# A selective-scan kernel: turning y between tiles, early weights and fillers in the head, last sums ahead of the last epilogue step, and one more step in the preparation of delta

## Chip, cores and metric

The kernel runs on one core of one Trainium2 chip. The metric is the device time of one execution in microseconds (us), as the median of several executions. In the profile, PE is TensorE, PEld its weight loads, DVE VectorE, ACT ScalarE, POOL GpSimd and SP SyncE; SPq is the queue of DMAs that SP issues.

## The reference, cut to what matters

The input is x [4, 64, 64, 96] in f32: four images, here called batches. A first block projects x to 2 x 192 channels with sign weights (`W_in`), puts one half through a 3x3 convolution of signs and a SiLU, and runs a selective scan over the 4096 pixels in four directions (by rows, by columns, and both reversed):

```
delta = softplus(delta + delta_bias)
dA = exp(dt[..., None] * A[None])
h  = dA * h + (dt * ut)[..., None] * Bt[:, :, None, :]
y  = einsum('bkdn,bkn->bkd', h, Ct)
return y + D[None, :, :, None] * u
...
inv_y = flip(out_y[:, 2:4], axis=-1)
y = out_y[:, 0] + inv_y[:, 0] + wh_y + invwh_y
y = (y - mu) / sqrt(var + 1e-05) * ln_w + ln_b
y = y * silu(z)
return bilinear(y, W_out, s_out, b_out)
```

h has 16 states for each of 192 channels. B, C and the input of delta are sign projections of the convolved image (`Wl`, then `Wd` for delta). Two column directions give y in transposed order (`wh_y`, `invwh_y`), so their sum has to be turned before it is added to that of the rows. Behind the block come an attention without softmax (its k and v are summed over all pixels of a batch before any output can be made) and a feed-forward layer whose operands are rounded to 8-bit floats.

## The kernel before, in words

**Work of a batch.** A batch is a *prologue*, 384 scan *pieces* and an *epilogue*.

- `prologue` (L539) takes group means, projects x (L647, L648), and convolves the signs in 16 parts of 512 pixels. A part is 15 matmuls L745 and one L786 that adds the input (`cz`); DVE and ACT finish it as u, stored to DRAM by rows (`ud`) and by columns (`utd`). Then the *rows stage* transposes the signs of u (`xa`, `xb`, L874), projects them with `wR` (`acc`, L940), and stores B and C (`bcd`, L952) and the signs for delta (`sgd`, L953). These are loaded again as `g` (L965) and turned (`gp`, L975) into `gT`.
- A piece is a tile [128 x 1024]: 32 channels by 4 of the 16 states, over 1024 pixels. The directions come in the order KORD = (1, 3, 0, 2), 96 pieces each: columns forwards and backwards, then rows. A batch is 384 pieces, the kernel 1536.
- The epilogue has `sums` (L1152) with eight tiles of 512 pixels (norm, gate, output projection, share of the attention's sums), `middle` (L1297), which makes a small matrix of the sums, and `last` (L1311), again eight tiles, which makes the output.

**The loop over pieces.** `Scans.run` (L1722) is an order written out by hand; step i issues:

1. `loads(i)`: B, C (`bc`, L1520) and delta (`dl`, L1531) by DMAs of 512 KB on SP; at every fourth piece the further summands of y (`load_sums`, L1611).
2. `carry(i-1)` (L1597), which keeps the last column of a scan, and `decay(i+1)` (L1554), exp of delta times A into PSUM, both on ACT. There are two decay buffers.
3. At every eighth step `evacuate(i-5)` (L1642): ACT copies finished y out of PSUM.
4. `reduce(i-4)` (L1628, L1633): PE sums products over the states into a bank of y; banks `y0` and `y1` alternate, one for every eight pieces.
5. `inject(i+3)`: POOL multiplies delta*u by B into a buffer `w`. `late_product`: POOL's product with C for an earlier piece, if it was left to POOL.
6. `scan(i)`: DVE's scan, and either DVE's product with C or none. Which engine takes the product is decided by `Tally` (helper L443), a running sum of estimated costs of each engine; it is kept from the start of the program.
7. DMA stores that are due, a step of `prepare`, and one step of the generator `back`.

`prepare` (L1450) makes a part of delta in steps, one per piece, starting at every eighth: matmuls L1489 into the bank of y that is not being summed, then Abs and Relu (L1494, L1495), Exp and Ln (L1497, L1498), a matmul L1502 that adds, DVE's product with u, ACT's copy L1508 out of the bank, and stores. The first reduce of the next eight pieces needs the bank free.

`back` (L491) runs all other work behind the pieces, one step at each: prologues of batches 1 to 3, epilogues of batches 0 to 2, and the *turns*. `turn(c, b)` (L994) loads the summed column directions of batch b in 16 tiles (`yt`), copies each in turned order on ACT (`yh`, L1015) and stores them in two DMAs (L1022). In `back` the turn of batch b+1 stands after all `sums` tiles of batch b, if its columns are nearly done by then, or else after the whole epilogue of b. The rows' directions of a batch need its turned y: when `run` comes to them (KORD 2) and it isn't turned, it runs `back` until it is, and issues no piece meanwhile.

**Head and tail.** For batch 0 the prologue runs alone, interleaved with `weights` (L163), a generator that loads, signs and transposes the weights; each of its transposes is a PE matmul into a y bank and a copy. `Scans.start` (L1668) then makes the first delta and its spread copies (`dl_s`, L1711). The last batch's epilogue runs alone too (`alone`), on two further lanes (`ln0`, `ln1`) and later a fourth (`l4`).

Of the kernel before, what the change touches and what calls it, by code (L numbers as in the profile page):

```python
# [25 lines left out]
CH = 1024  # L26
# [27 lines left out]
def hybrid_kernel(ctx: ExitStack, tc: tile.TileContext, a: dict, out: bass.AP):  # L54
# [108 lines left out]
    def weights():  # L163
# [39 lines left out]

        wi = temp("wi", [128, 3, DM], F32)
# [19 lines left out]
        wl = [temp(f"wl{o}", [128, DN], F32) for o in range(2)]  # L224
        for o in range(2):
            nc.gpsimd.memset(wl[o], 0.0)
            for kk in range(2):
                k, r0 = o + 2 * kk, 64 * kk
                nc.sync.dma_start(wl[o][r0 : r0 + 32, :], a["wl_bc"][32 * k : 32 * k + 32, :])
                nc.sync.dma_start(wl[o][r0 + 32 : r0 + 32 + NR, :], a["wl_dt"][k])  # L230
        wd = [temp(f"wd{x}", [128, NK, NR], F32) for x in range(2)]
        nc.sync.dma_start(wd[0], a["wd"][0:128])
        for r0 in (0, 64):
            nc.sync.dma_start(wd[1][r0 : r0 + 64], a["wd"][128:DN])
        wo = temp("wo", [DM, DN], F32)
        nc.sync.dma_start(wo, a["w_out"])
        small = {}
# [22 lines left out]
        nc.vector.tensor_tensor(sbx, pvx[:, :, B_X], pvx[:, :, MOVE0], ALU.add)  # L260
        wim = negmean("wim", wi, DM)
        wis = temp("wis", [128, 3, DM], BF16)
        for t in range(3):
            nc.scalar.activation(wis[:, t, :], wi[:, t, :], AF.Sign, bias=wim[:, t : t + 1])
        ps = transposed(winT, [wis[:, t, :] for t in range(3)])
        for x in range(2):
            nc.vector.tensor_copy(winB[:, 64 * x : 64 * x + 64], ps[0:DM, 128:DN], saturate=False)
        yield
        for i, cut in enumerate(cuts):
            nc.scalar.activation(cwA.rearrange("p t d -> p (t d)")[:, cut], cfa[i], AF.Sign, saturate=False)  # L270
            nc.scalar.activation(cwB[:, lines[i]], cfb[i], AF.Sign, saturate=False)
        yield

        part = temp("part", [96, 2, 2])
        for i in range(2):
            for h in range(2):
                nc.vector.tensor_reduce(part[:, h, i : i + 1], cwn[h][i], AX.X, ALU.add, apply_absolute_value=True)
            yield
        nc.vector.tensor_tensor(csc, part[:, :, 0], part[:, :, 1], ALU.add)
        nc.vector.tensor_scalar(csc, csc, 1.0 / (9 * DN), None, ALU.mult)  # L280

        nc.vector.tensor_tensor(cbias, pv[:, :, CONV_B], pv[:, :, RP0], ALU.add)
        nc.vector.tensor_tensor(acs, pv[:, :, PRELU], csc, ALU.mult)
        nc.vector.tensor_tensor(acb, pv[:, :, PRELU], cbias, ALU.mult)
        nc.vector.tensor_tensor(acb, acb, pv[:, :, B_X], ALU.add)
        nc.vector.tensor_tensor(acb, acb, pv[:, :, RP1], ALU.add)
        nc.vector.tensor_scalar(oma, pv[:, :, PRELU], -1.0, 1.0, ALU.mult, ALU.add)
        for h in range(2):
            nc.gpsimd.tensor_scalar(omad[:, h], i96, oma[:, h : h + 1], None, ALU.mult)
        yield  # L290

# [3 lines left out]
        kinds = (((0, 1), (2, None), (None, 0), (1, 2)), ((1, 0), (None, 2), (0, None), (2, 1)))  # L295
        for o in range(2):
# [5 lines left out]
            for kk in range(2):  # L302
                rows = slice(64 * kk, 64 * kk + 64)
                for x, pair in enumerate(kinds[kk]):
                    for half, j in enumerate(pair):
                        if j is not None:
                            to, src = we[rows, x, 64 * half : 64 * half + 64], sw[rows, 64 * j : 64 * j + 64]
                            if o:
                                to = we[rows, x, half::2]
                            else:  # L310
                                to, src = to.rearrange("p (e i) -> p i e", e=2), src.rearrange("p (i e) -> p i e", e=2)
                            nc.gpsimd.tensor_copy(to, src)
            yield
            yield
            transposed(wR[:, o].rearrange("p x m -> p (x m)"), [we[:, x, :] for x in range(4)])
            yield


        wdt = []
        for x, t in enumerate(wd):  # L320
            wdm = negmean(f"wdm{x}", t, NR)
            wds = temp(f"wds{x}", [128, NK, NR], BF16)
            for k in range(NK):
                nc.scalar.activation(wds[:, k, :], t[:, k, :], AF.Sign, bias=wdm[:, k : k + 1])
            wdt.append(temp(f"wdt{x}", [NR, NK * 32]))
            yield
            transposed(wdt[x].bitcast(F8), [wds[:, k, :] for k in range(NK)])
            yield
# [4 lines left out]
        for r0 in (0, 64):  # L333
            for s in range(8):
                at = r0 + NR * s
                nc.sync.dma_start(wdy.bitcast(F32)[at : at + NR, :, s, r0 // 4 : r0 // 4 + 16], two[:, :, 0:16])
        yield
        nc.vector.tensor_tensor(dbias, pvd[:, :, NK : 2 * NK], pvd[:, :, 2 * NK :], ALU.add)
# [3 lines left out]

# [3 lines left out]
        transposed(woutT.rearrange("p h m -> p (h m)"), [wos[:, 96 * h : 96 * h + 96] for h in range(2)])  # L346
        yield
        nc.vector.tensor_scalar(mean[:, 0], i96, -1.0 / DN, None, ALU.add)
        nc.vector.memset(mean[:, 1], -1.0 / DN)

        ones, diag = temp("ones", [96, 128]), temp("diag", [96, 4, 96])
        nc.vector.memset(ones, 1.0)
        for i in range(2):
            for h in range(2):
                col = pv[:, h, (LN_W, LN_B)[i] : (LN_W, LN_B)[i] + 1]
                nc.gpsimd.tensor_scalar(diag[:, 2 * i + h], i96, col, None, ALU.mult)
        yield
        ps = p.ps.tile([128, 512], F32, name="tpw", tag="y1")
        nc.tensor.matmul(ps[:, 0:384], ones, diag.rearrange("p i m -> p (i m)"), start=True, stop=True)
        for h in range(2):  # L360
# [8 lines left out]
        nc.vector.tensor_copy(  # L369
            back4.rearrange("p (x d) -> p x d", x=4), ident.rearrange("p (x d) -> p x d", x=4)[:, ::-1, :]  # L370
        )
# [11 lines left out]
        nc.vector.memset(on192, 1.0 / DN)  # L383
        nc.vector.memset(on96, 1.0 / DM)
        nc.vector.tensor_scalar(mean96, i96, -1.0 / DM, None, ALU.add)
        yield
        for name, dst in (("w1", w1q), ("w2", w2q), ("b1", b1q), ("b2", b2q)):
            q = dst if dst.dtype == F8 else temp(name + "q", list(dst.shape), F8)
            nc.vector.tensor_copy(q, small[name], saturate=False)
            if q is not dst:  # L390
                nc.vector.tensor_copy(dst, q)
        yield
        for k in range(NK):
            o, r0 = k % 2, 64 * (k // 2)
            nc.sync.dma_start(sbR[r0 : r0 + 32, o, 0:1], a["sl_bc"][0:32, k : k + 1])
            nc.sync.dma_start(sbR[r0 : r0 + 32, o, 1:2], a["bl_bc"][:, 32 * k : 32 * k + 32].rearrange("o p -> p o"))
            nc.sync.dma_start(sbR[r0 + 32 : r0 + 32 + NR, o, :], a["sl_dt"][k])
        yield
        al, al2 = temp("al", [128, 2, NK * NS]), temp("al2", [128, 2, 4, NK * NQ])
        nc.sync.dma_start(al, a["al"].rearrange("p h k s -> p h (k s)"))  # L400
        yield
        nc.scalar.activation(al, al, AF.Exp)
        nc.vector.tensor_scalar(al2, al.rearrange("p h (s j) -> p h j s", j=4), -1.0, None, ALU.mult)
        for g in range(NG):
            nc.sync.dma_start(anm[:, g, :], al2[32 * (g % 4) : 32 * (g % 4) + 32, g // 4])

    c = SimpleNamespace(**locals())
    c.ready, c.turned, c.later = set(), set(), Later(nc)
# [18 lines left out]
def load_x(c, b, xts):  # L427
    src = c.a["x"][b].rearrange("(i p) e -> p i e", p=128)
    for q, t in enumerate(xts):
        c.nc.sync.dma_start(t, src[:, 8 * q : 8 * q + 8, :])  # L430

# [40 lines left out]
def run(c):  # L472
# [6 lines left out]
    for _ in range(6):  # L479
# [11 lines left out]
    def back():  # L491
# [3 lines left out]
        for b in range(NB):  # L495
# [9 lines left out]
            if b + 1 < NB:  # L505
                if scans.done(b + 1, 2, 20):
# [21 lines left out]
    more.append(e.fourth_lane())  # L528

# [9 lines left out]
def prologue(c, b, xts=None):  # L539
# [11 lines left out]
    with tc.tile_pool(name=f"xg_{b}", bufs=1) as xgp:  # L551
# [3 lines left out]
        with tc.tile_pool(name=f"cv_{b}", bufs=1) as cvp:  # L555
# [23 lines left out]

            csum = bank("csum", 0)[0:1, 0 : 4 * DM]  # L580
# [153 lines left out]
            def alone_parts():  # L734

                mid = end = None
                for n, part in enumerate(parts + [None, None]):
# [4 lines left out]
                    for s in range(4):  # L742
# [17 lines left out]
                        elif s == 2:  # L760
                            if ahead:
                                next(ahead.pop(0), None)
                            if mid:
# [17 lines left out]
                    if part:  # L781
# [6 lines left out]
                        )  # L788
                        mid = (h, q, pz, v, r, nm)
# [65 lines left out]
        with tc.tile_pool(name=f"rw_{b}", bufs=1) as rw:  # L855
            xrs = rw.tile([128, 96, 64], BF16, name=f"xr_{b}", tag="xr")

            g2 = rw.tile([128, 2, 384], F8, name=f"g_{b}", tag="g")
            gw = g2.bitcast(F32)
# [6 lines left out]
            for o in (1, 0):  # L866
# [29 lines left out]

                for gh in range(2):
# [49 lines left out]
                    for kk in range(2):  # L947
                        k, r0 = o + 2 * kk, 64 * kk
                        for x, t in enumerate(tbcs):
                            n = L // 2 // len(tbcs)  # L950
                            at = L // 2 * gh + n * x
                            nc.sync.dma_start(c.bcd[b][k][:, at : at + n], t[r0 : r0 + 32, :])  # L952
# [3 lines left out]
                        )  # L956
                    if fast and gh == 0:
                        c.first_u()
                    yield
                c.later.flush()  # L960
                if o:
                    nc.gpsimd.memset(gw[:, :, 0:16], 0.0)
                    nc.gpsimd.memset(gw[:, :, 64:96], 0.0)
                for x, k in enumerate((o, o + 2)):
                    nc.sync.dma_start(gw[:, x, 16:64], c.sgd[b][k].rearrange("(p f) -> p f", p=128))  # L965
                    if fast and x:
# [873 lines left out]
```

## Time and profile before

| What | Value |
|---|---|
| Times of three runs, median | 5361.95 us (5360.22 to 5364.72) |
| The profiled execution | 5356.94 us |
| Its span, first to last instruction | 5355.2 us |
| Mean granted TensorE clock | 0.737 |
| First convolution matmul | 30.8 us |
| First scan | 180.2 us |
| POOL product, DVE scan, DVE product | 2.35, 2.34, 1.23 us |
| ACT decay | 1.12 us |
| ACT copy of the turn, L1015 | 1.07 us |

A line of the timeline gives start, duration, engine, source line, operation, output <- inputs, shapes and count (alike instructions next to each other are put together), and in brackets how long the engine had been idle before it and what ended that. A line of waits gives total, number and longest. The page's slices give the busy share in tenths of 40 equal pieces of the span, 134 us each. The granted clock is the share of full speed at which TensorE was allowed to run. Much of DVE's and POOL's work has the helper's line L443, so it is told apart by its tiles.

### The profile page before, as it was taken

Reading aid. Unit: us, or ns where it says so; the run is one execution under the profiler, and the core shown is the slowest. Engines: PE = TensorE matmul, PEld = TensorE weight load, DVE = VectorE, ACT = ScalarE, POOL = GpSimd, SP = SyncE. Lnnn points to the kernel's source line nnn. Section 1 sums busy time; section 2 is a strip of 40 time slices with the busy share of each in tenths; the row PEclk is TensorE's granted clock in tenths of the full one; section 3 lists DMA queues with packets and bytes.
Section 4 is the critical chain, followed back from the end, with each engine's and each line's share of the span. In section 5 each row is a group of like instructions: output and inputs, shape, how many; then the busy total and the mean of one; then the engine's idle time right before and its main releaser. Section 6 shows DMA issues by size and latency. Waiting matters only on the chain. (4 is left out here: it accounts for less than half of the span.)

```text
span 5355.2 us, 61897 instructions
## 1 busy us (share of the span) xinstructions
PE 3387.5 (63%) x20029; PEld 1351.6 (25%) x20029; DVE 5004.4 (93%) x3168; ACT 3606.7 (67%) x5644; POOL 4951.9 (92%) x2254
## 2 busy tenths in 40 slices
PE   7457665567645666566676556775666676664577
PEld 3212222122222222222222222222222222221223
DVE  4699999999999999999999999997999999999995
ACT  6577767687766666677777766666776666776554
POOL 4699999999999999999999999998999999999990
PEclk8667776678866877677777768776777776676788
DMA  5666666867766666766666666666666566667652
GB/s 107 189 194 197 212 189 203 260 203 211 222 195 182 205 218 203 230 208 204 216 204 193 193 207 224 195 198 222 201 204 211 189 209 202 200 190 233 217 177 65
DMA packets 605594, 1068.83 MB, mean 200 GB/s; under 512 B 219771, under 2 KB 336916, under 8 KB 603540
## 3 DMA queue, kind: packets, MB, share of 16 engines
q1 hardware_dynamic: 602884, 1063.93, 63.7%
q8 instruction: 157, 2.57, 0.2%
q14 instruction: 169, 1.38, 0.1%
q0 software_dynamic: 1536, 0.79, 0.1%
q10 hardware_dynamic: 848, 0.15, 0.0%
HBM read 829.69 MB, written 228.30 MB: 198 GB/s over the span
## 5 line engine op out<-in xcount | busy, mean ns | idle before, releaser
L443 POOL TENSOR_TENSOR w<-dl,bc 128x1024 f32<-128x1024 f32 x1524 | 3549.5, 2355 | 60.3 <-PE yp L1628 43.7
L1554 ACT ACTIVATE dA<-dl,anm 128x1024 f32<-128x1024 f32 x1524 | 1701.3, 1116 | 511.9 <-DVE w L443 319.0
L443 DVE TENSOR_TENSOR_SCAN dA<-dA,cy,w 128x1024 f32<-128x1024 f32 x726 | 1700.7, 2343 | 61.3 <-ACT dA L1554 50.1
L443 POOL TENSOR_TENSOR w<-h,bc 128x1024 f32<-128x1024 f32 x570 | 1341.4, 2353 | 100.5 <-DVE h L443 95.5
L1628 PE MATMUL yp<-w,sum 128*32 128x256 f32 x12288 | 1230.4, 500 | 157.4 <-ACT pd L1508 109.4
L443 DVE TENSOR_TENSOR w<-dA,bc 128x1024 f32<-128x1024 f32 x966 | 1183.3, 1225 | 63.8 <-DMA bc<-bcd 1.9
L443 DVE TENSOR_TENSOR_SCAN h<-dA,cy,w 128x1024 f32<-128x1024 f32 x426 | 996.8, 2340 | 3.4 <-ACT dA L1554 3.1
L1597 ACT COPY cy<-dA 128x1 f32<-128x1 f32 x723 | 114.2, 158 | 829.1 <-DVE w L443 828.1
L1628 PEld LDWEIGHTS yp<-w,sum 128*32 128x32 f32 x12288 | 320.0, 127 | 1218.4 <-issue 741.0
L443 DVE TENSOR_TENSOR_SCAN dA<-dA,w 128x1024 f32<-128x1024 f32 x240 | 547.7, 2282 | 50.8 <-ACT dA L1554 48.2
L443 DVE TENSOR_TENSOR_SCAN h<-dA,w 128x1024 f32<-128x1024 f32 x144 | 328.1, 2279 | 9.0 <-POOL w L443 8.6
L1489 PE MATMUL dps<-gT,wdz 128*128 128x64 fp8e5 x1008 | 115.5, 314 | 323.8 <-ACT ys L1642 313.8
L1502 PE MATMUL dps<-sp,ident 128*128 128x512 f32 x378 | 266.4, 793 | 73.1 <-ACT dps L1498 72.7
L1633 PE MATMUL yp<-ya,back 128*128 128x256 f32 x576 | 225.6, 511 | 0.0
L1489 PEld LDWEIGHTS <-wdz 128*128 128x128 fp8e5 x1008 | 94.5, 152 | 402.2 <-issue 401.3
L806 PE MATMUL cv<-tp,cwA 128*96 128x512 fp8e5 x432 | 160.2, 492 | 43.1 <-ACT r L838 41.8
L1597 ACT COPY cy<-h 128x1 f32<-128x1 f32 x429 | 79.9, 186 | 158.9 <-DVE h L443 158.6
L1489 PE MATMUL dps<-gT,wdy 128*128 128x64 fp8e5 x504 | 57.0, 312 | 183.1 <-ACT ys L1642 182.8
L1280 PE MATMUL kv<-wkv,tt 97*128 97x192 f32 x240 | 76.8, 491 | 136.9 <-DVE tt L443 136.9
L1494 ACT ACTIVATE pd<-dps,dbias,pvd 128x512 f32<-128x512 f32 x189 | 144.0, 762 | 20.9 <-PE dps L1489 20.6
L1143 PE MATMUL yc<-eys,mean 96*96 96x512 f32 x240 | 133.5, 708 | 35.6 <-DVE vks L443 21.4
L1633 PEld LDWEIGHTS yp<-ya,back 128*128 128x128 f32 x576 | 118.9, 238 | 119.3 <-issue 88.6
(380 smaller groups left out, 4559.2 us busy)
## 6 DMA issues: line engine op xcount, KB each, us to landing
dl<-dld SPq DMA_DIRECT2D x762, 512.0 KB
bc<-bcd SPq DMA_DIRECT2D x512, 512.0 KB
dld<-pd SPq DMA_DIRECT2D x126, 512.0 KB
yd<-ys SPq DMA_DIRECT2D x764, 64.0 KB
dld<-pd SPq DMA_DIRECT2D x126, 256.0 KB
ya<-yd SPq DMA_DIRECT2D x192, 128.0 KB
pu<-ud SPq DMA_DIRECT2D x32, 512.0 KB
pu<-utd SPq DMA_DIRECT2D x31, 512.0 KB
```

What stands on the lines that cost most here:

```text
L443: return getattr(self.eng, name)(out, *args, **kw)
L806: nc.tensor.matmul(ps, w[:, 96 * h : 96 * h + 96], tp[:, 8 * q + dy : 8 * q + dy + 8, dx : dx + IW], start=(w is taps[0][1]), stop=(w is t ...
L1143: self.c.nc.tensor.matmul(ps, w, x, start=(i == 0), stop=(i == len(pairs) - 1))
L1280: nc.tensor.matmul(pk[i // 2][:, i % 2], tt[:, 128 * i : 128 * i + 128], c.wkv, start=True, stop=True)
L1489: nc.tensor.matmul(pv[:, s], wd[:, k, s], gT[:, :, c0 : c0 + 16], start=(s == 0), stop=(s == 7))
L1494: nc.scalar.activation(d[:, 0], ps, AF.Abs, scale=sc, bias=bi)
L1502: nc.tensor.matmul(ps, c.ident, t, start=False, stop=True, skip_group_check=True)
L1554: c.nc.scalar.activation(t, self.dlt[i // NQ][0], AF.Exp, scale=c.anm[:, g, NQ * KORD[e] + q : NQ * KORD[e] + q + 1])
L1597: self.c.nc.scalar.copy(self.carries[g, q], h[:, CH - 1 : CH])
L1628: c.nc.tensor.matmul(y[32 * x : 32 * x + 32, g % 2, :], c.sum4, prod[:, 256 * x : 256 * x + 256], start=(q == 0), stop=(q == NQ - 1 and no ...
L1633: c.nc.tensor.matmul(y[:, g % 2, :], w, src, start=False, stop=(n == len(more) - 1))
```

## The change

1. **Turn between tiles.** A new method `between` is called by the main lane of `sums` and by `last` ahead of each tile. If the columns of the next batch are done, it turns them there.
2. **Head, weights.** The loads of `wl` and `wd` come first and on ACT's queue; their signs and transposes (`wR`, `wdt`) come before the first projections. `al` is loaded early; the loads of `sbR` and `anm` move up. The transposes of `woutT` and the matmuls `tpw` and `tpd` are deferred until all projections of the prologue are issued (`c.projected`). The 16 loads into `wdy` go to POOL's queue.
3. **Head, rows stage.** Stores of `sgd` go ahead of those of `bcd`. The first u and the first eight `bc` loads go to POOL's queue, right after the first half of the rows. Two memsets move up. The two tallies are set to zero when the pieces begin.
4. **Fillers.** `keep_busy` issues matmuls whose result nobody reads: 24 behind the last part of the convolution, 20 before the `gp` columns, 4, 2 and 2 in `middle` of the last batch and 4 and 3 in the first tile of `last`; 8 more ahead of the first group mean.
5. **End.** At the last piece `back` is not stepped, so the four last reduces and the last evacuation come ahead of the next epilogue step. By the instruction order, the main lane's tile 2 of the last batch is then made in the form for a lone epilogue, with two matmuls for the mean in place of eight.
6. **prepare.** One more `yield` between the matmuls L1489 and their use.

Cut to its core:

```diff
@@ weights
+                nc.scalar.dma_start(wl[o][r0 : r0 + 32, :], a["wl_bc"][32 * k : 32 * k + 32, :])
...
+        nc.scalar.dma_start(wd[0], a["wd"][0:128])
...
+        for x, t in enumerate(wds):
+            transposed(wdt[x].bitcast(F8), [t[:, k, :] for k in range(NK)])
...
+            if i == 0:
+                for o in range(2):
+                    transposed(wR[:, o].rearrange("p x m -> p (x m)"), [wes[o][:, x, :] for x in range(4)])
+                yield
...
+        while not c.projected:
+            yield
+        transposed(woutT.rearrange("p h m -> p (h m)"), [wos[:, 96 * h : 96 * h + 96] for h in range(2)])
@@
+def keep_busy(c, ps, n):
+    for _ in range(n):
+        c.nc.tensor.matmul(ps, c.identb, c.wR[:, 0].rearrange("p x m -> p (x m)"), start=True, stop=True)
@@ run
-    for _ in range(6):
+    for n in range(6):
+        if n == 4:
+            next(made)
         next(first)
@@ back
-                if scans.done(b + 1, 2, 20):
+                if b + 1 not in c.turned and scans.done(b + 1, 2, 20):
@@ prologue, rows stage
-                            nc.sync.dma_start(c.bcd[b][k][:, at : at + n], t[r0 : r0 + 32, :])
+                            rest.append((c.bcd[b][k][:, at : at + n], t[r0 : r0 + 32, :]))
...
+                    if not (fast and gh):
+                        for pair in rest:
+                            nc.sync.dma_start(*pair)
+                        rest.clear()
                     if fast and gh == 0:
                         c.first_u()
+                        c.loads_ahead()
...
+                if fast:
+                    keep_busy(c, c.p.ps.tile([128, 512], F32, name="warm_rw", tag="y1"), 20)
...
-                    if fast and x:
-                        c.loads_ahead()
@@ Epilogue
+            if ln is self.lane:
+                yield from self.between()
...
+    def between(self):
+        b = self.b + 1
+        if not self.alone and b < NB and b not in self.c.turned and self.scans.done(b, 2):
+            yield from turn(self.c, b)
@@ Scans.prepare
         yield
+        yield
@@ Scans.first_loads
-        for w, to in enumerate((self.bt, self.ct)):
-            for q in range(NQ):
-                self.load_bc(w, to, 0, 0, 0, q)
+        for w, q in ((0, 0), (1, 0), (0, 1), (0, 2), (0, 3), (1, 1), (1, 2), (1, 3)):
+            self.load_bc(w, (self.bt, self.ct)[w], 0, 0, 0, q, self.c.nc.gpsimd)
@@ Scans.run
+        c.vec.us = c.gps.us = 0.0
...
-            next(back, None)
+            if i < n - 1:
+                next(back, None)
```

## Prediction

> **What bounds the kernel now.** I read the busy shares first, then the slices, then the waits, and last the timeline of every stretch in which VectorE (DVE) stood still.
>
> ```profile
> PE 3387.5 (63%) x20029; PEld 1351.6 (25%) x20029; DVE 5004.4 (93%) x3168; ACT 3606.7 (67%) x5644; POOL 4951.9 (92%) x2254
> DVE  4699999999999999999999999997999999999995
> POOL 4699999999999999999999999998999999999990
> ```
>
> DVE and GpSimd (POOL) are both full from the third slice to the last but one: 1536 pieces at about 3.27 us each, with POOL products of 2.35 us, DVE scans of 2.3 and DVE products of 1.23. An edit shortens the kernel only if it takes DVE and POOL idle time away, or shortens the head (before the pieces) or the tail (after them). There are three such places: slices 1 and 2, the 7 in the middle, and the last slice.
>
> The middle one, from the timeline around 3670 us:
>
> ```profile
> 3670.24 7.72 ACT L1015 COPY yh<-yt 96x512 f32<-96x512 f32 x8 [8.83 <-DMA yt<-yd]
> 3679.14 2.30 DVE L443 TENSOR_TENSOR_SCAN dA<-dA,w 128x1024 f32<-128x1024 f32 x1 [23.96 <-ACT dA L1554]
> 3681.08 2.36 POOL L443 TENSOR_TENSOR w<-dl,bc 128x1024 f32<-128x1024 f32 x1 [20.05 <-PE yp L1628]
> ```
>
> The turn's copies stand in ScalarE's (ACT) queue ahead of the next decay, waiting for loads. DVE stops for 24.0 us, POOL for 20.1. It is the only turn of the four that does so.
>
> The head, from the timelines of TensorE (PE), SyncE's queue (SP), ACT and DVE:
>
> ```profile
> 86.54 1.46 PE L745 MATMUL cv<-tp,cwB 128*96 128x512 fp8e5 x6
> 97.43 0.59 PE L786 MATMUL cz<-xsT,winT 96*96 96x512 fp8e5 x1 [9.44 <-DVE u L443]
> ...
> 157.65 1.03 PE L975 MATMUL gp<-ident,g 128*128 128x128 fp8e5 x8 [11.30 <-DMA g<-sgd]
> ...
> 156.86 5.67 SPq L1520 DMA_DIRECT2D bc<-bcd x8
> ...
> 175.98 2.15 ACT L1554 ACTIVATE dA<-dl_s,anm 128x1024 f32<-128x1024 f32 x2 [7.24 <-DMA dl_s<-w_s]
> ...
> 191.50 2.29 DVE L443 TENSOR_TENSOR_SCAN h<-dA,w 128x1024 f32<-128x1024 f32 x1 [6.28 <-POOL w L443]
> ```
>
> The convolution has 16 parts, each with one L786 matmul, and these start at 36.58, 41.31, 49.20, 58.42, 62.33, 70.91, 79.93, 83.84, 97.43, 103.94, 107.86, 111.86, 117.20, 120.68, 124.51 and 127.98. Undisturbed parts come 3.9 us apart, which 15 intervals would make 58.7; they take 91.4. The excess of 32.7 is weight preparation run between the parts.
>
> The tail, from PE's timeline and a table by stretches (busy us of PE, PEld, DVE, ACT, POOL with counts; clock; DMA):
>
> ```profile
> 5236.83 6.85 PE L1143 MATMUL yc<-eys,mean 96*96 96x512 f32 x8 [2.86 <-DVE vks L443]
> 5243.61 1.93 PE L1628 MATMUL yp<-w,sum 128*32 128x256 f32 x32
> ```
>
> ```profile
> 5285.00:5312.00 27.00, 23.59 (x33) 6.56 (x34) 9.04 (x18) 10.33 (x17) 0.00 (x0) 0.56 0.27 79
> 5312.00:5332.00 20.00, 17.07 (x83) 9.25 (x82) 12.96 (x26) 15.00 (x26) 0.00 (x0) 1.00 0.11 30
> ```
>
> The last sums of y wait behind 6.8 us of an epilogue tile, and the first round of the last layer runs at half clock.
>
> **The turn.** In the instruction order the third turn moves from pieces 1055–1057, where 14 of its copies form one burst, to 975–994, a copy per piece, and the fourth from 1406–1425 to 1358–1377. What 16 spread copies cost can be read from the turns that are spread already: in the 20 pieces of the first turn DVE's idle gaps over 0.05 us sum to 1.8 us, in those before and after to 2.5 and 0.9; in the fourth to 0, against 1.6 before it. So the copies of 1.07 us hide under ACT's idle third, and the 16 loads and 2 stores on SP come some 60 pieces before y is needed. Without that cover they cost at most 16 x 1.07 = 17 us again. The stall goes: the 10 pieces around it took 54.9 us instead of 33, so **−22** (20 to 24). Next due is only the following decay.
>
> **The head up to the convolution's end.** The transposes of wR and wdt go ahead of the first projection, and the work behind `al` (the 9.44 above: DVE waits for an ACT copy of it, which waits for its load) starts earlier. The intervals that end at 41.31, 49.20, 58.42, 97.43, 103.94 and 117.20 lose their excess: 0.8 + 4.0 + 5.3 + 9.7 + 2.6 + 1.4 = 23.8. Those ending at 70.91 and 79.93 hold the transposes of woutT, tpw and tpd (4.7 + 5.1), which the change only defers to when all projections are done, near part 11; I keep their cost. So −24 (−30 if they fit there, −12 if half of it returns). Against it, the early work stands before the first projection (24.01 us): eleven weight loads issued by ACT with waits, 2.6 us of signs, two copies of 0.68 and two of 0.42: +5 (+3 to +9).
>
> **From rows to the first pieces.** The sgd stores went out at 152.03 and 154.24 behind bcd stores; in front of them they leave some 3.5 us earlier. But the 8 bc loads (512 KB each) now start ahead of the g loads, on POOL's queue, and share the engines with these: I take −2 (−4 to +3). In return bc is out of the way when dl_s loads: those took 8.2 us to the first decay at a DMA share of 1.0 (158 to 180 us); at 5 us less crowding −4 (0 to −6). The Trainium skill, "DMA: Bandwidth & Descriptors", section "Issuing engine by pattern", speaks against this queue: a simple load belongs on Sync, GpSimd being slower, some 0.4 us to the first byte by the page's figures. The trace has 5.67 us for 8 issues on SP, 0.71 each, and 0.49 each for POOL's three xg issues. By the page +0.4 once, by the row nothing, since POOL is idle then; I take the row. The tallies set to zero give the first pieces' products to DVE: the waits of 6.28 and 2.32 us on POOL before scans 2 and 3 shrink by about −3.5. Fillers: 24 wide matmuls after the last part at 0.3 us (the bf16 pair of 512 columns took 0.59) are 7 us under PE's idle 7.4 before xa; 20 are 6 to 11 us (0.55 each at the slow clock) under the 11.3 shown: nothing, at worst +5.
>
> Head: −24 + 5 − 2 − 4 − 3.5 = **−28** (−10 to −40).
>
> **The tail.** With the reduces ahead of the epilogue step they start at 5236.8 instead of 5243.6: −6.8. The main lane's tile 2 of the last batch then takes the short mean, with up to 3.9 us of yc, sy and var less before the means of lanes 0 and 1: −10.7 in all; its eight additional DVE operations (0.64, 0.43, 0.74, 0.69, twice each) are 5.0 us, of which 3.5 on the path. Clock: fv takes 2.02 us at 5289 and 1.10 at 5321. Twelve such pairs lie in the slow stretch, 11 us; half is then covered by DVE and ACT, so −5.5. Here a rule disagrees with the row. The Trainium skill, "TensorE: Matmul & The Clock Gate", section "Part 1: The HAM clock gate", lets the clock drop after an idle window of about 3.4 us and return after a busy one of that length. In the row PE idles 0.8 us at a time at most, is 87% busy, and stays at 0.56 for 27 us. By the rule no gap asks for fillers: gain 0, cost 15 x 0.3 less PE's 2.9 us of gaps, +2. By the row density decides, and fillers buy 5.5. I take the row, less the cost. Tail: −10.7 + 3.5 − 5.5 + 2 = −10.7, taken as **−10** (−2 to −17).
>
> **The steady pieces.** Four more products on DVE: 4 x 1.23 = +5. Pieces whose decay must wait out a scan (about 65 gaps of 1.25 us) are 62 in the new order: −4. The additional step in prepare moves the copy L1508 one step (3.3 us) later, in ACT's queue, and the reduces behind it on PE:
>
> ```profile
> PE yp L1628 <- ACT pd L1508: 109.4, 29, 7.0
> ```
>
> Where that bank's reduce began less than 3.3 us after the copy it slips, 1.8 us on average. A late reduce hurts only if POOL then waits for its w buffer; carrying each slip against the slack to the inject nine pieces later, 13 of about 190 pay, 12 us in all; with one buffer more, none. I take +3 (0 to +12). ACT's wait of 20.6 us for PE before L1494 goes, but ACT is not the bound: 0. Together **+4**.
>
> **Sum.** −22 − 28 − 10 + 4 = −56. The profiled execution took 5356.94 us (span 5355.2): 5301. The median, 5361.95, stands 5.0 above it: **5306**.
>
> **Rivals.**
> 1. *The head gives little.* For it: the page of slices has DMA at 0.5 to 0.7 here, and new ACT issues precede everything. If early loads cost +9, half the excess returns (−12), and g is late by 3, the head is −12+9+3−4−3.5 = −7.5: 5326.
> 2. *Slower: the late copy empties the ring of w buffers.* If the slack is one step shorter than I count, the same sum gives 67 late injects and 88 us: 5306 − 3 + 88 = 5391. It decides from 0.3 us per prepare (59 / 189). Against it: POOL's waits for yp are 43.7 us now, 20 of them in the one stall.
> 3. *The fillers don't do what they say*: the clock stays at half, or they stand before needed matmuls: tail −4, rows +3: 5315.
> 4. *The turn's copies only move the stall*: −5 instead of −22: 5323.
>
> **How the numbers follow.** Forecast 0.60 (5288 to 5318), rival 1 0.15, rival 2 0.05, rival 3 0.10, rival 4 0.04, a head and tail at their best ends (5280) 0.06. Range 5280 to 5330. About 0.2% (11 us) is what the measurement tells from no change. Faster 0.94; the same 0.03, where several rivals meet; slower 0.03, rival 2 less the part of it that stays under the others' gain.
>
> **What would show it.** Right: no DVE gap over 10 us after 205; first scan near 155 to 160; L786 intervals of 3.9 except two; last reduces right after the last product; clock near 1.0 through the first round. Wrong: POOL waiting over 60 us for yp, or the intervals still above 5.

## The result, and the profile after

The changed kernel takes 5290.6 us (median; 5288.3 to 5294.7) against 5361.1 us before, a ratio of 0.9868 (95% interval 0.9851 to 0.9885), so 70 us less. 5306 was forecast, with 5280 to 5330 as the range. The profiled execution took 5288.32 us, its span 5286.5, which is 68.6 us less than before.

From the page after, busy shares and slices of 132 us:

```profile
PE 3427.5 (65%) x20089; PEld 1358.7 (26%) x20092; DVE 5011.1 (95%) x3178; ACT 3606.5 (68%) x5644; POOL 4956.0 (94%) x2277
...
DVE  5799999999999999999999999999999999999996
...
POOL 5799999999999999999999999999999999999991
```

The 7 in the middle of DVE's row is a 9, and the second slice went from 6 to 7; busy times grew by 7 and 4 us. What was taken away is idle time.

I lay the starts of equal scans side by side and get this account (a minus is earlier than before):

| Stretch | Before | After | Change | Forecast |
|---|---|---|---|---|
| Start to the convolution's first L786 (after: L804) matmul | 36.58 | 42.26 | +5.7 | +5 |
| From there to the last of the 16 | 91.4 | 67.0 | −24.4 | −24 |
| From there to the first scan | 52.2 | 52.2 | 0.0 | −6 |
| First scan to scan 5 | 21.6 | 17.9 | −3.7 | −3.5 |
| Scans 1050 to 1100, with the turn | 186.3 | 161.5 | −24.8 | −22 |
| All other pieces | | | −8.1 | +4 |
| Last product to the end | 118.5 | 105.2 | −13.3 | −10 |

The head after, from the timelines of PE and DVE:

```profile
109.26 0.38 PE L804 MATMUL cz<-xsT,winT 96*96 96x512 fp8e5 x1
109.48 5.34 PE L440 MATMUL warm_cv<-wR,identb 128*128 128x512 bf16 x23
...
136.71 0.62 PE L1008 MATMUL gp<-ident,g 128*128 128x128 fp8e5 x8 [2.11 <-DMA g<-sgd]
141.41 0.61 PE L1008 MATMUL gp<-ident,g 128*128 128x128 fp8e5 x4 [4.07 <-DMA g<-sgd]
...
161.47 2.30 DVE L453 TENSOR_TENSOR_SCAN dA<-dA,w 128x1024 f32<-128x1024 f32 x1
```

The fillers lie where PE waited. But there are now two waits for g, where there was one of 11.3 us before. The queue of SP shows that nothing stood between the two loads before, and four bcd stores after:

```profile
155.79 1.03 SPq L965 DMA_DIRECT2D g<-sgd  x2
```

```profile
130.86 0.35 SPq L1000 DMA_DIRECT2D g<-sgd  x1
131.30 1.97 SPq L1020 DMA_DIRECT2D bcd<-tbc  x4
133.37 0.46 SPq L1000 DMA_DIRECT2D g<-sgd  x1
```

From the last L786 or L804 matmul to the first gp matmul it is 29.7 us before and 27.5 after, so the first g gained 2.2 us. At the matmuls of the first delta (`dA_s`), which stand behind the second g, nothing is left of it: 32.3 before, 33.0 after.

The tail after, from PE's timeline and the table by stretches (span; busy of PE, PEld, DVE, ACT, POOL with counts; clock; DMA):

```profile
5181.39 0.64 PE L1681 MATMUL yp<-w,sum 128*32 128x256 f32 x8 [1.07 <-DVE w L453]
5181.96 1.13 PE L1686 MATMUL yp<-ya,back 128*128 128x256 f32 x4
5182.93 1.88 PE L1178 MATMUL mu<-eys,on 96*96 96x512 f32 x4
```

```profile
5222.00:5250.00 28.00, 23.74 (x93) 10.23 (x93) 15.51 (x32) 16.86 (x29) 0.00 (x0) 1.00 0.38 112
```

The last reduce waits for nothing but DVE's last product, and the short mean (`mu`, four matmul records where `yc` had eight) stands behind it. The first round of the last layer has its full clock.

And the waits (total, times, longest), before:

```profile
DVE dA L443 <- ACT dA L1554: 98.3, 66, 24.0
```

and after:

```profile
PE yp L1681 <- ACT pd L1561: 306.7, 96, 9.1
...
DVE dA L453 <- ACT dA L1607: 66.1, 56, 2.2
```

The wait of 24.0 us is gone. PE waits 307 us for the later copy instead of 109, yet the pieces became shorter. The experiments ask why.

### The profile page after: what moved, and what is told of

It is laid out like the page before. It is cut to its first block, busy times and chain, and to the rows that moved or that the text cites. A ratio compares the mean times of both kernels' runs of the same rounds, so it can differ in the third digit from the quotient of the medians.

```text
span 5286.5 us, 61986 instructions
## 1 busy us (share of the span) xinstructions
PE 3427.5 (65%) x20089; PEld 1358.7 (26%) x20092; DVE 5011.1 (95%) x3178; ACT 3606.5 (68%) x5644; POOL 4956.0 (94%) x2277
## 5 line engine op out<-in xcount | busy, mean ns | idle before, releaser
L453 POOL TENSOR_TENSOR w<-dl,bc 128x1024 f32<-128x1024 f32 x1524 | 3550.2, 2357 | 46.7 <-PE yp L1681 28.1
L1555 PE MATMUL dps<-sp,ident 128*128 128x512 f32 x378 | 295.4, 873 | 110.2 <-ACT dps L1551 110.0
L1178 PE MATMUL sy<-eys,meanw 96*96 96x512 f32 x232 | 133.0, 708 | 34.4 <-ACT eys L1263 34.4
L1178 PE MATMUL yc<-eys,mean 96*96 96x512 f32 x232 | 137.2, 746 | 24.8 <-DVE vks L453 16.4
L1548 ACT ACTIVATE sp<-dps,dbias,pvd 128x512 f32<-128x512 f32 x189 | 144.6, 765 | 0.0
```

The costliest lines, as they stand in the source:

```text
L453: return getattr(self.eng, name)(out, *args, **kw)
L1178: self.c.nc.tensor.matmul(ps, w, x, start=(i == 0), stop=(i == len(pairs) - 1))
L1548: nc.scalar.activation(t, ps, AF.Relu, scale=sc, bias=bi)
L1555: nc.tensor.matmul(ps, c.ident, t, start=False, stop=True, skip_group_check=True)
```

## The experiments

My theory after the result was that the terms add up as in the table, and that the 8 us in the other pieces came with the moved turn or with prepare's step. The rival was that those pieces depend on the exact order of instructions, and on no single part. "Pieces" below is the time from scan 20 to scan 1530 (before 4966.3 us, after 4933.6), and "tail" the time from the last product to the end.

Two scatters bear on what follows. Single runs of one kernel lie up to 15 us apart (those of the changed kernel between 5288 and 5295), so medians that differ by 5 us or less are not told apart. And a profile shows one run: with the same order of pieces they took 4932.9 to 4937.7 us in seven profiles, and with the same head the first scan came at 160.6 to 164.7 in six.

**The turn alone.** The kernel before, with `between` and its calls, and nothing else.

```diff
+            if ln is self.lane:
+                yield from self.between()
```

> The kernel before with the turn between tiles alone. My theory, that the stall of 24 us simply goes and that the spread copies hide on ACT: the span is 22 to 25 us shorter than the 5355 of before, the starts of the pieces run level with those of before up to piece 1050 and are some 24 us earlier from 1100 on, no DVE gap above 4 us in the pieces. If the turn also gave the further 8 us that the changed kernel gains between pieces 1300 and 1400 (its epilogue then lies elsewhere), 30 to 33 us shorter. The rival, that the copies only move the stall: at most 10 us shorter, with new DVE gaps in pieces 975 to 995.

Measured: 5343.9 us, ratio 0.9972 (0.9965 to 0.9980), only 14 us less. At its place the turn gave what was forecast: level with before at piece 1050, and 24.0 us earlier at piece 1100. By piece 1300 only 10.5 us were left. The timelines of DVE, and for the second place of PE too, show some of what came in between:

```profile
4182.56 0.69 DVE L443 TENSOR_TENSOR pd<-dps,pu 128x512 f32<-128x512 f32 x1 [2.31 <-PE dps L1511]
```

```profile
4285.02 4.39 PE L1143 MATMUL yc<-eys,mean 96*96 96x512 f32 x5
...
4289.92 1.13 PE L1511 MATMUL dps<-sp,ident 128*128 128x512 f32 x2
...
4291.08 0.69 DVE L443 TENSOR_TENSOR pd<-dps,pu 128x512 f32<-128x512 f32 x1 [3.14 <-PE dps L1511]
```

The moved turn shifts the epilogue that follows it. At three pieces DVE, whose next instruction is prepare's product, waits 2.3, 1.5 and 3.1 us for `dps`; at the second place shown, the epilogue's `yc` stands on PE ahead of prepare's matmul. Between pieces 1100 and 1300, where 13.6 us are lost, the rest is mostly in waits for decays, 10 us against 4, with seven short gaps instead of three, of which more below. So the rival "the copies move the stall" was wrong, but "next due is only the following decay" was wrong too.

**Prepare's step taken out of the changed kernel, and added alone to the kernel before.**

```diff
         yield
-        yield
         kind = part // 2
```

> The changed kernel without the additional step of prepare. My prediction put the later copy at +3 us (0 to 12): without the step the kernel would be about 3 us faster, PE's wait for pd near 110 us instead of 307, and POOL's wait for yp down from 28 to about 23. The other theory, that this step is what made the steady pieces 8 us shorter, since ACT no longer waits for PE there: 8 us slower, with ACT's wait for dps back near 20 us and some 8 more DVE gaps of 1.25 us. If the gaps are only a matter of how orders happen to fall, within 5 us either way with no fixed sign.

> The kernel before with the additional step of prepare alone. The turn alone gave some 12 us instead of 24, with DVE waiting 1.5 to 3.1 us for prepare's chain (pd) at three pieces, and taking the step out of the changed kernel cost 12 to 16. My present theory: the step gives prepare's chain more time wherever epilogue or prologue work on PE comes in between, so it gains by itself, but the kernel before had only 1.3 us of such waits: 0 to 5 us faster, and the step's worth shows only together with the moved turn. The rival, that the step is worth the same everywhere (ACT's 20 us of waits for PE's dps): 12 to 16 us faster. The prediction's +3 with its risk of +12: slower.

Without the step, 5302.7 us (ratio 0.9897, 0.9882 to 0.9912), 12 more than with it; the pieces are 16 us longer. Waits of DVE for `dps` of 2.6, 1.7 and 1.4 us are back (5 us more in all), short gaps take 4 us more, and some 8 us are waits of DVE's products for loads of C:

```profile
DVE w L453 <- DMA bc<-bcd: 9.7, 5, 4.6
```

and with the step

```profile
DVE w L453 <- DMA bc<-bcd: 1.4, 1, 1.4
```

Why C comes late there stays open; in the seven profiles with the changed kernel's pieces these waits are 1.4 to 6 us, so part of the 8 is scatter. The step alone: 5342.8 us (0.9968, 0.9955 to 0.9980), 18 us less than before, with pieces 15 us shorter although the turn's stall was still there, at 26.4 us. Here short gaps take 21 us less, and the waits for `dps` are as before. My theory of that moment (0 to 5 us) fell: the step is worth some 15 us in both kernels, by different waits, and its sign is the opposite of my forecast. It also covers what the moved turn brought: pieces 1100 to 1300 take 649.5 us before and in the changed kernel, 663.1 with the turn alone, and 655.4 without the step.

**One more step still,** the slower rival: one more `yield`, so that the copy comes later again.

> The changed kernel with one more step in prepare again, so that ACT's copy of pd comes one step of 3.3 us later still. This is the slower rival of the prediction made on purpose: with the slack one step shorter the sum over slips gave 67 late injects and 88 us. If that sum is right, 60 to 100 us slower, with POOL's wait for yp above 80 us. If the w buffers still cover it: within 5 us, POOL's wait for yp below 45. The theory that each further step only helps by taking waits off DVE: up to 5 us faster.

```profile
POOL w L453 <- PE yp L1682: 44.4, 39, 4.1
```

```profile
PE yp L1682 <- ACT pd L1562: 693.8, 170, 13.0
```

Measured: 5320.6 us (0.9928, 0.9916 to 0.9941), 30 us more than the changed kernel, with pieces of 4963.1. PE waits for nearly every copy, but POOL for only 44 us where it waited 28. So the w buffers cover most of it, and my price of 88 us with 67 late injects was three to five times too high. The direction was right, but for two steps more and not for one. In DVE's idle time most of the 30 us is found again: 10 more in waits for loads of C, 6 in short gaps, 4 for `dps`, 6 in smaller gaps.

**The short gaps.** They look like this, in the timeline of the kernel before:

```profile
3722.52 0.14 ACT L1597 COPY cy<-dA 128x1 f32<-128x1 f32 x1
...
3723.31 1.12 ACT L1554 ACTIVATE dA<-dl,anm 128x1024 f32<-128x1024 f32 x1 [0.65 <-DVE h L443]
...
3724.53 2.30 DVE L443 TENSOR_TENSOR_SCAN dA<-dA,w 128x1024 f32<-128x1024 f32 x1 [1.25 <-ACT dA L1554]
```

The decay of a piece starts when the scan ahead has ended, not beside it, and DVE stands for one decay. These are decays that follow a carry in ACT's queue, carry a wait for DVE of their own, and come after a product on DVE and then one on POOL. Such decays can be counted in a kernel's instruction order, and the gaps of 1.0 to 1.4 us right ahead of a scan (pieces 21 to 1530) in its trace:

| Kernel | Counted in the order | Gaps in the trace | Their sum, us | Pieces, us |
|---|---|---|---|---|
| before | 65 | 60 | 74.7 | 4966.3, with a stall of 24 |
| turn alone | 67 | 60 | 74.8 | 4956.4 |
| step alone | 56 | 43 | 53.9 | 4951.0, with a stall of 26 |
| changed, without the step | 64 | 55 | 68.7 | 4949.6 |
| changed | 62 | 52 | 64.8 | 4933.6 |
| changed, one step more | 73 | 57 | 71.3 | 4963.1 |
| changed, tallies kept | 50 | 39 | 48.9 | 4919.8 |

In all 14 kernels there are 5 to 16 fewer gaps than counted decays, and in the seven with the same order of pieces 50 to 52. Nearly all gaps lie at counted decays: 57 of the 60 before, 50 of the 52 after. The wait of its own tells such a decay from its likes without exception: of the decays after piece 20 that follow a carry, a DVE product and a POOL product, the 64 that have one all started after the scan ahead had ended, and the 356 that have none all started beside it (61 and 352 in the changed kernel). So this loss is fixed by the order. In the kernel before 23 of the gaps fell on the last of eight pieces, with the step alone 6. Why the order gives one decay a wait of its own and spares another, I did not settle.

**The tallies kept.**

```diff
-        c.vec.us = c.gps.us = 0.0
```

> The changed kernel without the reset of the two tallies. The first scan stays at 161.5; the first products go back to POOL, and scans 2 and 3 wait for POOL's injects again: scan 5 comes 3 to 4 us later than now (17.9 us behind the first). If the loss stays, the end is 3 to 4 us later; if POOL and DVE make it up later because the tally then only shifts the same work, 0 to 2.

```profile
DVE dA L453 <- ACT dA L1607: 59.2, 47, 2.5
```

Measured: 5278.4 us (0.9849, 0.9835 to 0.9862), 12 us less than the changed kernel; its profiled execution is 11 less. The start behaves as expected: scan 5 is 2.8 us later, although scan 0 is 0.9 earlier. But the pieces are 14 us shorter, which I had not expected. The other split of products gives 12 fewer decays of the bad kind and 13 fewer gaps, 16 us of idle time; smaller gaps took 2.5 us back. The reset buys 3.7 us at the start and pays 14 for them in the pieces.

**The rows stage.** First, bc behind the g loads, still on POOL's queue.

```diff
                     if fast and gh == 0:
                         c.first_u()
-                        c.loads_ahead()
...
+                    if fast and x:
+                        c.loads_ahead()
```

> The changed kernel with the first eight bc loads issued behind the two g loads as before, still on POOL's queue. If bc is what delays g (the stage from the last part of the convolution to the first scan took 52.2 us both before and after): the second g comes about 4 us earlier, DVE's first sum of delta 3 to 5 us after the last part earlier than now (38.4 us behind it now), but dl_s then loads beside bc, so the first scan gains 0 to 4 us. If bc is not what delays g: the same arrival of g, and dl_s some 3 us later, so the first scan is 3 us later.

Measured: 5285.6 us (0.9867, 0.9853 to 0.9880). The g loads land as before (the gp matmuls wait 1.1 and 4.7 us), and the first scan is at 160.9 instead of 161.5, as the convolution ended 0.4 earlier. That is inside the scatter: where bc stands among the loads shows no effect. Next, both g loads ahead of the bcd stores left over:

```diff
+                for x, k in enumerate((o, o + 2) if fast else ()):
+                    nc.sync.dma_start(gw[:, x, 16:64], c.sgd[b][k].rearrange("(p f) -> p f", p=128))
                 for x, k in enumerate((o, o + 2)):
-                    nc.sync.dma_start(gw[:, x, 16:64], c.sgd[b][k].rearrange("(p f) -> p f", p=128))
+                    if not fast:
+                        nc.sync.dma_start(gw[:, x, 16:64], c.sgd[b][k].rearrange("(p f) -> p f", p=128))
```

> The changed kernel with both g loads issued ahead of the remaining bcd stores. Theory: the matmuls of the first delta stand on PE behind the gp columns of the other direction, whose g load is issued behind bcd stores and lands 4.1 us after the first; so both g first brings the first delta's matmuls, and DVE's first sum of delta, 4 to 5 us earlier, and the first scan 2 to 5 us earlier (dl_s may take part of it back at a full DMA). The rival, that the queues of DMA are so full that g lands at the same time whatever is issued between: no change.

```profile
136.52 0.62 PE L1011 MATMUL gp<-ident,g 128*128 128x128 fp8e5 x8 [1.86 <-DMA g<-sgd]
138.15 0.38 PE L1011 MATMUL gp<-ident,g 128*128 128x128 fp8e5 x4 [1.02 <-ACT gT L1019]
...
138.60 1.48 PE L1743 MATMUL dA_s<-gT,wdz 128*128 128x64 fp8e5 x16
```

The wait for the second g is gone, and the first scan comes 3.8 us earlier (157.6), 48.3 us behind the last L804 matmul. With the stores between, nine profiles have 51.0 to 55.1 there. So the changed kernel lost there by its own order: bcd stores were put between the two g loads, and on PE the first delta's matmuls stand behind the gp columns of the second. In the whole: 5287.4 us (0.9865, 0.9852 to 0.9879), 3 us less, which can't be told from the scatter. In the profiles the lead was gone by piece 1000. However, the changed kernel's own profile is the odd one there: between scans 900 and 1000 it gains 2.5 to 3.3 us on four of the six others with the same pieces, and 1 on the other two. How much of the 3.8 us survives stays open.

**The fillers of the head left out, and the deferral left out.**

```diff
-                            keep_busy(c, c.p.ps.tile([128, 512], F32, name="warm_cv", tag="y1"), 24)
...
-                    keep_busy(c, c.p.ps.tile([128, 512], F32, name="warm_rw", tag="y1"), 20)
```

> The changed kernel without the 24 and 20 fillers of the head. The clock of TensorE was 0.8 to 0.6 there before and xa's 32 matmuls took 3.60 us, gp's eight 1.03; with the fillers 2.47 and 0.62. If the fillers hold the clock: back to those values and the first scan 1.5 to 3 us later. If they only fill PE's waits and the clock comes with the faster convolution: no change in these, and the first scan within 0.5 us. If they stand in the way: 0.5 to 2 us earlier.

```profile
115.29 3.26 PE L900 MATMUL xa<-ident,xg 128*128 128x128 fp8e5 x32 [6.12 <-DMA xg<-sg]
...
135.72 1.03 PE L1004 MATMUL gp<-ident,g 128*128 128x128 fp8e5 x8 [10.09 <-DMA g<-sgd]
```

xa and gp are back at about their slow durations, so the fillers do hold the clock (0.83 against 0.56 from 127 to 137 us). But the first scan is no later without them (1.4 us earlier, inside the scatter of the head), and the time is the same, 5291.5 us (0.9876, 0.9861 to 0.9891): what PE gains there, it spends waiting for the loads of `xg` and `g`, as the 6.12 and 10.09 us show.

```diff
-        while not c.projected:
-            yield
```

> The changed kernel without the wait for the end of the projections, so that the transposes of woutT, tpw and tpd come between the early parts of the convolution again. There they cost 4.7 and 5.1 us of excess before; deferred they show 1.0 and 2.3 us above the undisturbed part. If it is the y banks, held by the projections, that made them dear: the convolution is 5 to 7 us longer and the first scan as much later. If they are dear only behind late weight loads: within 1 us.

5299.8 us (0.9893, 0.9876 to 0.9909), 9 more than the changed kernel. The convolution starts 1.8 us earlier, takes 73.8 us instead of 67.0, and the first scan is 3.8 later. So the transposes are dear beside the projections, though these only make up a part of the 9 us; the rest, in the pieces and the tail, is no more than profiles scatter.

**The end: fillers left out, and the old order.**

```diff
-        busy(4)
...
-        busy(2)
...
-        busy(2)
...
-                    c.busy(4)
...
-                c.busy(3)
```

> The changed kernel without the 15 fillers of the last epilogue. My theory, that density decides the clock and that the fillers hold it: the clock falls to about 0.5 for some 20 us behind the first matmul of the last layer, fv takes 2.0 us, and the end comes 4 to 6 us later. The rule that only an idle window of about 3.4 us lowers the clock: no gap there is near that long, so the clock stays at 1.0 and the end comes 0 to 2 us earlier. A third case: the clock's windows have shifted with the shorter path, and it stays full without them.

PE's timeline, and its table by stretches:

```profile
5228.33 0.38 PE L1178 MATMUL m<-wff,m 96*96 96x96 f32 x2 [0.78 <-DVE m L453]
5229.03 0.45 PE L1178 MATMUL m<-m,wqT 96*97 96x96 f32 x2 [0.32 <-ACT m L1348]
5229.83 2.02 PE L1178 MATMUL at<-tt,m 97*96 97x512 f32 x2 [0.35 <-DVE m L453]
5232.63 2.02 PE L1178 MATMUL fc<-x,mean 96*96 96x512 f32 x2 [0.78 <-DVE x L453]
5235.33 2.02 PE L1178 MATMUL fv<-fq,on 96*96 96x512 f32 x2 [0.68 <-ACT fq L1407]
```

```profile
5222.00:5250.00 28.00, 21.66 (x58) 8.96 (x59) 7.90 (x17) 9.37 (x18) 0.00 (x0) 0.70 0.44 120
```

5296.0 us (0.9884, 0.9871 to 0.9898), 5 more, which the medians alone don't settle. The tail is 111.7 us; in the changed kernel it is 105.2, and in the eight runs whose tail is unchanged 102.7 to 107.8. The clock falls at `at` without an idle time over 1.1 us in the 10 us ahead, and stays low until 5246. With 15 fillers in those gaps it doesn't fall. All profiles agree: the first matmuls of `fv` take 1.17 and 1.06 us in the four kernels without fillers at the end (before, turn alone, step alone, this one) and 0.67 and 0.59 in the ten with them. By the rule that the prediction weighs (the Trainium skill, "TensorE: Matmul & The Clock Gate", section "Part 1: The HAM clock gate"), which is the second case of this expectation, the clock would have stayed full. So no single idle window decides here, but how PE's time is filled; the runs don't tell the share of busy time from the kind of matmul, as the fillers are wide and in bf16.

```diff
-            if i < n - 1:
-                next(back, None)
+            next(back, None)
```

> The changed kernel with the epilogue stepped at the last piece as before, so that the last reduces stand behind a step of the main lane again. By my account the order is worth 6.8 us of waiting and up to 3.9 of shorter work less 3.5 of DVE's: the time from the last product to the end goes from 105.2 to some 111 (109 to 113), and POOL and DVE in the pieces do as before. If the last reduces were not what the tail waits for: 105.

```profile
5186.27 5.37 PE L1178 MATMUL yc<-eys,mean 96*96 96x512 f32 x8 [2.66 <-DVE vks L453]
5191.56 1.93 PE L1681 MATMUL yp<-w,sum 128*32 128x256 f32 x32
```

5293.2 us (0.9881, 0.9867 to 0.9896), with a tail of 113.6: the order is worth 8.4 in the profiles, against 6.8 + 3.9 − 3.5 = 7.2 by the forecast. But this profile is of the slowest of its four runs (5301.4 us), and the median moved by only 3. That the last reduces wait again is shown; how much of the 8.4 a usual run loses is not.

**The better version:** tallies kept and both g loads first.

> The changed kernel with the tallies kept and both g loads first, the two edits that look better than the change. The number of decays that follow a carry with a wait for DVE of their own is 50 in its instruction order, as with the tallies kept alone (62 in the changed kernel): so about 45 gaps of 1.25 us, and the 11 us of that run stay. The g loads bring the first scan to 157; whether their 3.8 us survive to the end is the question, since with the changed kernel they were gone by piece 1000: if time won in the head is kept unless such gaps differ, 15 us faster than the changed kernel; if POOL and DVE swallow it, 11.

5274.8 us, ratio 0.9844 (0.9830 to 0.9859), 16 less than the changed kernel and the lowest median of all. Its profiled execution took 5273.83 us, 14.5 less. The pieces have 38 gaps (counted: 50), with the tallies alone 39. The first scan is at 155.7, 4.8 us ahead of the run with the tallies alone, and 1.2 of it were left at the last piece, so again the lead of the head mostly went in the pieces. What the order of the loads adds to the kept tallies, 4 us in the medians, is not told from the scatter.

**What no run took apart.** The early weight loads were not tested alone, so the 24 us of the convolution are read from the starts of its parts before and after.

## Why the prediction was right, and where not

**The three places** were right. Idle time went at the turn, in the head and in the tail, and DVE and POOL are still the bound.

**The turn, −22:** −24.8 at its place. In the whole it is worth 14 alone, as an epilogue that lies elsewhere brings new waits. That "next due is only the following decay" was the wrong step there; prepare's step covers those waits, so the changed kernel keeps the gain.

**The convolution, −24 and +5:** −24.4 and +5.7, but partly by errors that cancel. I kept 9.8 us for the deferred transposes, and they show 3.3. I let the other parts lose all excess, and 5.0 us remain there, in waits of 0.6 to 1.5 us for DVE's u at every other part.

**Rows to first scan, −6:** 0.0. Two terms failed. The −2 for sgd ahead of bcd came at the first g (2.2) and was lost at the second: I saw bc as what could crowd out g, but it was the bcd stores between the two g loads, and PE's order behind the second. And the −4 for dl_s did not come: from its first issue to the first inject it took 11.1 us before, while the DMA engines moved 284 GB/s, and 10.4 after, while they moved 148 with bc out of the way. So bc beside it was not what made it long; what does stays open. That bc went by POOL's queue cost nothing that shows (0.59 us an issue, against 0.71 on SP before); what the first byte took there no run shows. Fillers at nothing was right.

**The reset, −3.5:** −3.7 at the start, but net about +12 by the run without it. I took it for a matter of the first pieces. It sets the split of products throughout, and I had counted the consequence (62 against 65) without asking what the count would be without it (50).

**The later copy, +3:** the sign was wrong; it is worth some −15. The slips on POOL were sized rightly (outside the stall 23.6 us before, 28.1 after). What failed is that the term has nothing but these slips in it: what the step does for DVE stood at 0, with the reason that ACT is not the bound. ACT makes the decays that DVE waits for, and with the step DVE waits less: alone by 21 us of short gaps, in the changed kernel by 4 of short gaps, 5 for `dps` and up to 8 for C. Whether ACT's own 20.6 us of waits for PE had a part in that is not shown.

**The tail, −10:** −13.3. The clock is the term that was too small: fillers were to bring 5.5 − 2 = 3.5, and leaving them out costs 6.5 in the profiles and 5 in the medians. The Trainium skill's rule for the clock, weighed there, would have had nothing or a loss.

**The rivals and the signs.** The head gave 22 of the 28, so less, but far from the 7.5 of rival 1, and the fillers did what they say. Of the signs of being wrong, one came in part: three intervals between L804 matmuls are above 5 us (5.1, 5.7 and 6.2, the last with deferred transposes in it). The slower rival did not come, since with one step the w buffers cover the slip; with two it comes as +30.

The sum of −56 fell 13 us short of −69: the steady pieces are 12 better than forecast, the tail and the turn 3 each, and the rows stage 6 worse. That the total lies nearer to the forecast than its terms do is luck in part; but neither error alone would have carried it out of the range.

## What to carry to other kernels

An engine that isn't the bound still counts where the bound engine waits for its next result: a step more of distance between producer and user was worth more here than the waits on its own engine suggested, and one more step than that lost it twice. Where two engines share products by a running cost, any edit of that cost moves the whole order, so count the bad patterns in the new order, and in the order with each part taken out. And a store put between two loads of one stage delays whatever stands behind the second load in another engine's queue; here that was 3.8 us at the first scan, of which no more than scatter was left at the end.

## What the runs showed of the hardware that was not expected

The clock of TensorE fell to 0.50 at a stretch in which PE was never idle for more than 1.1 us but busy in short matmuls, and did not fall when 15 wide matmuls filled the gaps (0.70 against 1.00 over 28 us, with the same split in all 14 profiles). Raising it in the head from 0.56 to 0.83 brought no time that could be measured.
